# Graph layer with gathered edges: block 0's messages before the weight set-up, and b_e as the opening pass of the edge products

## The chip, the cores and the metric

One Trainium2 chip, of which the program uses one core. The metric is device time in microseconds for one execution of the whole program. Three timed runs of the kernel before are shown; a fourth execution was taken with the hardware profiler and is the one that all rows of the profile come from.

## The reference, cut to what matters

Nodes: N = 8192 rows of C = 256. Edges: E = 131072, sorted by destination, each with 64 attributes. In a few lines:

```python
ea  = edge_attr @ w_e + b_e                      # 131072 x 256
msg = relu(x[src] + ea)                          # one gathered row of x for each edge
agg = segment_sum(msg, dst, num_segments=8192)
t   = x + agg
h_local = bn(relu(t @ w1 + b1) @ w2 + b2 + x)
h_attn  = bn(attention(x in 256 groups of 32 nodes, 4 heads) @ out_w.T + out_b + x)
out = h_local + h_attn
out = bn(out + relu(out @ m_w1 + m_b1) @ m_w2 + m_b2)
result = layernorm(x + out)
```

Everything is float32.

## The kernel before, in words

**Edge blocks.** The edges are cut into NB = 128 blocks of 1024. A block passes through these steps:

- `gather(b)` (issue at L138): eight indirect DMAs from GpSimd's queue (POOL), one for each 128 edges. They write the rows `x[src]` into the tile `xs`, of which there are four buffers. The indices of blocks 0 and 1 lie in the small tile `srcd`, those of all later blocks in `srci`, which is made in the set-up (L193 to L198).
- `load_edges(b)` (L154): four loads of edge attributes into `ea` from SyncE's queue (SP), two buffers. `edge_transpose(b)` (L169, VectorE) turns them into `eaT`, two buffers.
- `edge_products(b)` (L459 and L467, TensorE): `edge_attr @ w_e`, in two halves of one `pe` tile each. A `pe` tile takes two banks of PSUM; the index `i` of the code selects both the bank and which 64 partitions of `eaT` and `w_e` the product is taken over. In the blocks below NX = 20 a second set of matmuls, L467, adds `b_e`: its stationary operand `sel` has ones in row 0 and in row 64 and zeros elsewhere, and its moving operand is `be`. From block 20 on, the gathers read `xb` instead, a copy of x to which `b_e` has been added, and L467 is left out.
- `edge_messages(b)` (L487 VectorE, L491 ScalarE): `msg = relu(pe + xs)`. When L487 has read `xs`, its buffer is free for `gather(b + 4)`.
- `edge_hot`, `edge_sums` (L496, L510), `edge_place` (L528, L538): the sum over destinations by matmuls with one-hot operands.

**Nodes.** 16 chunks of 512 nodes. `attention_front` loads `xn` (L276), transposes it (L283) and makes q and k (L294); `attention_back` and `dense` (L308 to L444) do the rest. The copy `xb` is made in blocks 0 to 14 of the loop: SyncE loads `xp`, VectorE adds `b_e` (L558), SyncE stores it (L559).

**Order.** The program text fixes the order on TensorE everywhere, and on VectorE and ScalarE in the first NV = 26 blocks. The loop over pairs of blocks takes, for the pair (b, b+1): the gathers of blocks b+2 and b+3; products and messages of b; the sums of the pair before; products and messages of b+1; then steps of the node streams, dealt out by assumed costs (`PER_X` = 4.2 and `PER` = 5.1 for each block). Before the loop stands the set-up: the loads of indices and weights, their transposes (L197 to L266), and the transposes of the first two node chunks. Matmuls of block 0 come after all of that. The last 24 blocks are ordered by a table of arrival times, `came`, which assumes 10.06 us for each block.

**Queues.** Loads of `w_e`, `b_e`, `in_w` and `out_w` are issued by ScalarE (L179 to L188), all others by SyncE. As built, the loads from SyncE and ScalarE share eight semaphores in turn, so a load is issued only when the eighth load before it has landed; the gathers have eight of their own, in the same way.

Of the kernel before, what the change touches and what calls it, by code (L numbers as in the profile page):

```python
# [9 lines left out]
FP = mybir.dt.float32  # L10
I32 = mybir.dt.int32
AF = mybir.ActivationFunctionType
ALU = mybir.AluOpType
# [40 lines left out]
def gnn_kernel(ctx: ExitStack, tc: tile.TileContext, x, src, dst, edge_attr, w, out):  # L54
# [72 lines left out]
    def bank2():  # L127
        return pps.tile([P, 2, CH], FP, name="pe", tag="pe", bufs=2)
# [31 lines left out]
    load_edges(0)  # L160
    gather(1)
    load_edges(1)
# [3 lines left out]
    def edge_transpose(b):  # L166
        ea = ea_of.pop(b)
        eaT = eaT_of[b] = epool.tile([P, NH * EQ, QR], FP, name="eaT", tag="eaT", bufs=2)
        nc.vector.transpose(eaT, ea[:, QR:].rearrange("p (g d) -> p g d", d=ED)[:, :, :QR])  # L169

    with tc.tile_pool(name="setup", bufs=1) as sp:


        srci_r = npool.tile([P, BE], I32, name="srci_r", tag="y")
        dsti_r = npool.tile([P, BE], I32, name="dsti_r", tag="h1")
        nc.sync.dma_start(srci_r, src.rearrange("(s e) -> s e", s=NB))
        nc.sync.dma_start(dsti_r, dst.rearrange("(s e) -> s e", s=NB))
        for h in range(2):
            nc.scalar.dma_start(we[h * ED : (h + 1) * ED, :], w["w_e"])  # L179
        nc.scalar.dma_start(be, w["b_e"][None, :].to_broadcast([P, C]))  # L180
        in_r = npool.tile([P, 3 * KC, C], FP, name="in_r", tag="m1")
        out_r = npool.tile([P, KC, C], FP, name="out_r", tag="vn")
        nc.scalar.dma_start(in_r, w["in_w"].rearrange("(o p) c -> p o c", p=P))
# [4 lines left out]
        nc.scalar.dma_start(out_r, w["out_w"].rearrange("(o p) c -> p o c", p=P))  # L188
        for b in range(2):
            edge_transpose(b)  # L190
            load_edges(b + 2)
        srcf = npool.tile([P, NH * TJ, EQ, QR], FP, name="srcf", tag="zT")
        nc.vector.tensor_copy(srcf, srci_r.rearrange("s (t r m) -> s t m r", r=QR, m=EQ))  # L193
        for h in range(NH):
            ps = bank()[:, : TJ * NB].rearrange("p (j s) -> p j s", j=TJ)
            for j in range(TJ):
                nc.tensor.transpose(ps[:, j, :], srcf[:, h * TJ + j].rearrange("s m r -> s (m r)"), ident)  # L197
            nc.vector.tensor_copy(srci[:, :, h * TJ : (h + 1) * TJ].rearrange("p s j -> p j s"), ps)  # L198

# [74 lines left out]
    def attention_front(n0, st, pool, bank):  # L274
        xn = st["xn"] = pool.tile([P, TN, C], FP, name="xn", tag="xn", bufs=4)
        nc.sync.dma_start(xn, x[ds(n0, CH), :].rearrange("(t p) c -> p t c", p=P))  # L276
        yield REST
# [170 lines left out]
    chunk = [{} for _ in range(NCH)]  # L448
    pe_of, msg_of, oh_of, newest = {}, {}, {}, {}

    def edge_products(b):

        eaT = eaT_of.pop(b).rearrange("p (h m) r -> p h (m r)", h=NH)
        for h in range(0, NH, 2):
            pe = bank2().rearrange("p i (u c) -> p i u c", u=2)
            for u in range(2):
                for i in range(2):
                    rows = slice(i * ED, (i + 1) * ED)
                    nc.tensor.matmul(  # L459
                        pe[:, i, u, :], eaT[rows, h + u], we[rows, :],  # L460
                        start=(b >= NX or u == 0), stop=(b >= NX), skip_group_check=True,
                    )
            if b < NX:
                for u in range(2):
                    for i in range(2):
                        rows = slice(i * ED, (i + 1) * ED)
                        nc.tensor.matmul(  # L467
                            pe[:, i, u, :], sel[rows, :], be[rows, :], start=False, stop=True, skip_group_check=True
                        )
            pe_of[b, h] = pe  # L470

    def next_edges(b):
        if b < NB:
            edge_transpose(b)
        if b + 2 < NB:
            load_edges(b + 2)

    def edge_messages(b):

        xs = xs_of.pop(b)  # L480
        msg = msg_of[b] = epool.tile([P, NH, TJ, C], FP, name="msg", tag="msg", bufs=3)
        n = 2 if b < NB - 1 else 1
        for h in range(0, NH, 2):
            pe = pe_of.pop((b, h))
            for u in range(0, 2, n):
                hs = slice(h + u, h + u + n)
                nc.vector.tensor_add(  # L487
                    msg[:, hs].rearrange("p u i c -> p i u c"), pe[:, :, u : u + n, :],
                    xs[:, hs].rearrange("p u i c -> p i u c"),
                )  # L490
                nc.scalar.activation(msg[:, hs], msg[:, hs], AF.Relu)  # L491

    def edge_hot(b):

        oh = oh_of[b] = epool.tile([P, TB, WN], FP, name="oh", tag="oh", bufs=2)
        nc.vector.tensor_tensor(  # L496
            oh,
            iota_n[:, None, :WN].to_broadcast([P, TB, WN]),
            rel[:, b, :, None].to_broadcast([P, TB, WN]),
            ALU.is_equal,  # L500
        )

    def edge_sums(blocks):

        pw = pps.tile([P, 2, C], FP, name="pw", tag="pw", bufs=1)
        for i, b in enumerate(blocks):
            msg, oh = msg_of.pop(b), oh_of.pop(b)
            for j in range(TJ):
                for h in range(NH):
                    nc.tensor.matmul(  # L510
                        pw[h * WN : (h + 1) * WN, i, :], oh[:, h * TJ + j, :], msg[:, h, j, :],
                        start=(j == 0), stop=(j == TJ - 1), skip_group_check=True,
                    )
        n = len(blocks)
        ws = epool.tile([P, 2, C], FP, name="ws", tag="ws", bufs=2)
        newest["ws"] = nc.scalar.copy(ws[:, :n], pw[:, :n]).ins  # L516
        oh2 = epool.tile([P, 2, WB], FP, name="oh2", tag="oh2")
        for i, b in enumerate(blocks):
            nc.vector.tensor_scalar(oh2[:, i, :], iota_n, wrow[:, b : b + 1], None, ALU.is_equal)
        return blocks, ws, oh2  # L520

    def edge_place(blocks, ws, oh2):

        l2 = pps.tile([P, KC, C], FP, name="l2", tag="pw", bufs=1)
        last = len(blocks) - 1
        for i in range(last + 1):
            for k in range(KC):
                nc.tensor.matmul(  # L528
                    l2[:, k, i * NPB : i * NPB + WB], ws[:, i, k * P : (k + 1) * P], oh2[:, i, :],
                    start=(i == 0 and k == 0), stop=(i == last), skip_group_check=True,  # L530
                )
        n = blocks[0] * NPB - WL
        end = n + last * NPB + WB
        for c in range(max(n, 0) // CH, (min(end, N) - 1) // CH + 1):
            assert chunk[c]["v"]
            a, z = max(n, c * CH), min(end, (c + 1) * CH)
            xT = chunk[c]["xT"][:, :, a - c * CH : z - c * CH]
            newest["xT"] = nc.vector.tensor_add(xT, l2[:, :, a - n : z - n], xT).ins  # L538

# [86 lines left out]
    with tc.manual_schedule(engines={PE}):  # L626
# [9 lines left out]
        for c in range(NCH):  # L636
            st, before, same = chunk[c], chunk[c - 1], chunk[c - 4]
            front = attention_front(c * CH, st, npool, bank)
            if c < 2:
                next(front)  # L640
                next(front)
# [23 lines left out]
        while b < TAIL:  # L665
# [10 lines left out]
            edge_products(b)  # L676
            next_edges(b + 2)
            edge_messages(b)
# [188 lines left out]
```

## Time and profile before

| | us |
|---|---|
| timed runs | 1328.47, 1331.11, 1333.70 |
| median | 1331.11 |
| the profiled execution | 1331.09 |
| its span, first to last instruction | 1329.3 |
| TensorE busy in the span | 1195.2 (90%) |
| GpSimd busy | 983.9 (74%) |
| VectorE busy | 784.9 (59%) |
| ScalarE busy | 587.7 (44%) |
| mean granted TensorE clock | 0.967 |

How to read it: all rows of the profile count time from the first instruction of the span, and the profiled execution adds 1.8 us around the span. In a row of the timeline the first number is the start, the second the time from there to the end of the row, both in us, then come the engine, the line of the kernel, the operation, output and input, shapes and count; in brackets stands the idle time of the engine just before and what ended it. "issue" means that the engine waited for nothing that the profile shows. A float32 matmul leaves two matmul records and two weight loads. The share of busy time of an engine tells little here, since the set-up, the blocks below 20, the long middle and the end have different limits.

### The profile page before, as it was taken

The numbers are of one execution on the slowest core, as the hardware profiler recorded it, in microseconds if no ns is written. First come the engines' busy times: TensorE is split into PE (matmuls) and PEld (weight loads), VectorE is DVE, ScalarE is ACT, GpSimd is POOL, SyncE is SP. The second block draws the span as 40 slices with busy tenths as digits, with TensorE's granted clock in tenths as the row PEclk, the third lists the DMA queues.
The fourth block names the chain that finished last, engine by engine and source line by source line (L and its number), as shares of the span: only waits on it lengthen the run. The fifth ranks groups of instructions, "written<-read, shape, count | busy, mean of one in ns | idle before, by whom it ended". The sixth has DMA issues, their size and how long they took to land.

```text
span 1329.3 us, 21099 instructions
## 1 busy us (share of the span) xinstructions
PE 1195.2 (90%) x7795; PEld 741.0 (56%) x7795; DVE 784.9 (59%) x1339; ACT 587.7 (44%) x840; POOL 983.9 (74%) x1032
## 2 busy tenths in 40 slices
PE   2898989999998989899898988989898999999987
PEld 1566656556555556555555555545555555545655
DVE  4377555765756565755647465465646557575654
ACT  1343433454536454443435444354454444443433
POOL 6677777777777777777777777777777777777771
PEclk9899999999999989999999999989899999999998
DMA  7999966676667666666756666566566466656741
GB/s 204 320 267 299 260 199 169 169 199 167 181 160 196 157 181 167 171 177 165 190 150 185 160 176 171 157 181 167 170 169 199 138 169 186 166 163 159 192 129 47
DMA packets 148904, 240.34 MB, mean 181 GB/s; under 512 B 27934, under 2 KB 112188, under 8 KB 148028
## 3 DMA queue, kind: packets, MB, share of 16 engines
q0 software_dynamic: 49152, 134.28, 37.6%
q1 hardware_dynamic: 97196, 103.34, 28.9%
q10 hardware_dynamic: 2448, 1.32, 0.4%
q8 instruction: 63, 1.03, 0.3%
q14 instruction: 45, 0.37, 0.1%
HBM read 222.06 MB, written 16.78 MB: 180 GB/s over the span
## 4 chain that ended last, share of the span: by engine, by line
PE 38%; POOL 28%; issue 14%; DVE 9%; DMA 8%; ACT 2%; DVEq 0%; ACTq 0%; SPq 0%; POOLq 0%
POOL xs L138 28%; PE at L391 11%; PE pe L459 8%; DMA xs<-xb,srci 5%; PE at L294 5%; PE pw L510 4%; DVE msg L487 3%; PE l L528 3%; PE at L372 2%; PE pe L467 2%; PE at L308 1%; DMA xp<-in_x_dram 1%; PE at L360 1%; PE pe L325 1%; DMA in_r<-in_L_gnn_in_w_dram 1%
## 5 line engine op out<-in xcount | busy, mean ns | idle before, releaser
L138 POOL DMA_INDIRECT xs<-xb,srci x864 | 823.7, 953 | 263.2 <-issue 250.1
L491 ACT ACTIVATE msg<-msg 128x1024 f32<-128x1024 f32 (+1 forms) x258 | 270.0, 1049 | 435.5 <-DVE msg L487 432.6
L487 DVE TENSOR_TENSOR msg<-pe,xs 128x1024 f32<-128x1024 f32 (+1 forms) x258 | 305.7, 1199 | 155.4 <-DMA xs<-xb,srci 88.6
L459 PE MATMUL pe<-we,eaT 64*128 64x256 f32 x2048 | 271.0, 398 | 29.8 <-DVE msg L487 26.4
L459 PEld LDWEIGHTS pe<-we,eaT 64*128 64x128 f32 x2048 | 192.1, 191 | 118.5 <-issue 74.6
L138 POOL DMA_INDIRECT xs<-in_x_dram,srci x144 | 143.0, 993 | 48.8 <-issue 39.6
L169 DVE STREAM_TRANSPOSE eaT<-ea 128x512 f32<-128x512 f32 x128 | 90.1, 704 | 99.6 <-PE pe L459 70.9
L510 PE MATMUL pw<-msg,oh 128*32 128x256 f32 x2048 | 130.4, 389 | 6.6 <-DVE oh L496 5.0
L391 PE MATMUL at<-hA,mw 128*128 128x512 f32 (+2 forms) x304 | 123.9, 538 | 2.9 <-DVE hA L401 2.2
L294 PE MATMUL at<-xT,inT 128*128 128x512 f32 x256 | 120.9, 598 | 0.4 <-ACT xT L284 0.4
L391 PE MATMUL at<-m,mw 128*128 128x512 f32 (+2 forms) x304 | 117.5, 529 | 2.5 <-ACT qk L297 2.2
L510 PEld LDWEIGHTS pw<-msg,oh 128*32 128x32 f32 x2048 | 60.4, 111 | 69.1 <-issue 30.7
L528 PEld LDWEIGHTS l<-oh,ws 128*128 128x128 f32 x512 | 78.0, 196 | 28.4 <-issue 21.9
L528 PE MATMUL l<-oh,ws 128*128 128x160 f32 x512 | 87.9, 312 | 2.0 <-ACT ws L516 2.0
L391 PEld LDWEIGHTS at<-hA,mw 128*128 128x128 f32 x304 | 54.7, 196 | 50.5 <-issue 42.6
L391 PEld LDWEIGHTS at<-m,mw 128*128 128x128 f32 x304 | 54.2, 190 | 49.9 <-issue 44.5
L538 DVE TENSOR_TENSOR xT<-l,xT 128x96 f32<-128x96 f32 (+4 forms) x107 | 46.1, 452 | 54.2 <-PE l L528 53.9
L294 PEld LDWEIGHTS at<-xT,inT 128*128 128x128 f32 x256 | 47.0, 190 | 55.3 <-issue 51.0
L391 PE MATMUL at<-xT,w 128*128 128x512 f32 (+2 forms) x152 | 70.9, 606 | 6.9 <-DVE xT L538 6.9
L407 ACT ACTIVATE m<-at,vec 128x512 f32<-128x512 f32 (+2 forms) x76 | 46.8, 616 | 57.2 <-PE at L391 56.7
L297 ACT ACTIVATE qk<-at,vec 128x512 f32<-128x512 f32 x64 | 43.6, 684 | 62.6 <-PE at L294 62.4
L391 PE MATMUL at<-h,w 128*128 128x512 f32 (+2 forms) x152 | 64.2, 544 | 6.1 <-ACT h L398 6.1
(107 smaller groups left out, 1199.9 us busy)
## 6 DMA issues: line engine op xcount, KB each, us to landing
ea<-in_edge_attr_dram SPq DMA_DIRECT2D x512, 128.0 KB
xs<-xb,srci POOLq DMA_INDIRECT x864
xn<-in_x_dram SPq DMA_DIRECT2D x16, 512.0 KB
out_dram<-y SPq DMA_DIRECT2D x14, 512.0 KB
xp<-in_x_dram SPq DMA_DIRECT2D x10, 512.0 KB
xb<-xp SPq DMA_DIRECT2D x10, 512.0 KB
xp<-in_x_dram SPq DMA_DIRECT2D x3, 1024.0 KB
xb<-xp SPq DMA_DIRECT2D x3, 1024.0 KB
```

Source lines behind the costliest of these rows:

```text
L138: nc.gpsimd.indirect_dma_start(out=xs[:, h, j, :], out_offset=None, in_=x if b < NX else xb[:, :], in_offset=bass.IndirectOffsetOnAxis(ap= ...
L169: nc.vector.transpose(eaT, ea[:, QR:].rearrange("p (g d) -> p g d", d=ED)[:, :, :QR])
L294: nc.tensor.matmul(ps, inT[:, k, o * P : (o + 1) * P], xT[:, k, :], start=(k == 0), stop=(k == KC - 1))
L297: nc.scalar.activation(qk[:, o, :], ps, AF.Identity, bias=v_("in_b", o))
L391: nc.tensor.matmul(ps, wt[:, k, o * P : (o + 1) * P], act[:, k, :], start=(k == 0), stop=(k == nk - 1))
L407: nc.scalar.activation(m1[:, o, :], layer(mw1, KC, o, hA), AF.Relu, bias=v_("m_b1", o))
L459: nc.tensor.matmul(pe[:, i, u, :], eaT[rows, h + u], we[rows, :], start=(b >= NX or u == 0), stop=(b >= NX), skip_group_check=True,)
L487: nc.vector.tensor_add(msg[:, hs].rearrange("p u i c -> p i u c"), pe[:, :, u : u + n, :], xs[:, hs].rearrange("p u i c -> p i u c"),)
L491: nc.scalar.activation(msg[:, hs], msg[:, hs], AF.Relu)
L510: nc.tensor.matmul(pw[h * WN : (h + 1) * WN, i, :], oh[:, h * TJ + j, :], msg[:, h, j, :], start=(j == 0), stop=(j == TJ - 1), skip_group_ ...
L528: nc.tensor.matmul(l2[:, k, i * NPB : i * NPB + WB], ws[:, i, k * P : (k + 1) * P], oh2[:, i, :], start=(i == 0 and k == 0), stop=(i == la ...
L538: newest["xT"] = nc.vector.tensor_add(xT, l2[:, :, a - n : z - n], xT).ins
```

## The change

Five things change; the work computed is the same.

1. **Block 0 ahead of the weights.** `edge_products(0)`, `next_edges(2)` and `edge_messages(0)` are taken out of the loop and put into the set-up, after `srci` is made and before the transposes of `in_w`. For this the functions on edges are moved up in the file, unchanged but for `edge_products`.
2. **Order of loads.** All set-up loads are now issued by SyncE, in this order: `src`, the edges of block 0, `w_e`, the edges of block 1, `b_e`, `dst`, twelve small vectors, `in_w`, chunk 0 of x, `out_w`, chunk 1 of x, edges of blocks 2 and 3.
3. **Set-up on VectorE.** The index conversion (`srcf`, four copies to `srci`) now stands ahead of `edge_transpose(0)` and `(1)`. VectorE's two adds of block 0's messages stand between the steps that prepare `dst`.
4. **Chunks 0 and 1 of x** are loaded by a new function `load_nodes`, ahead of their transposes.
5. **b_e first, in passes of 512 columns.** In a half of a block below 20, `b_e` opens the sum with one matmul of 512 columns for each 64 partitions (`be` repeated twice by a step of zero), and the four products of 256 columns are added to it. Before, four products of 256 columns opened it, and four `b_e` matmuls of 256 columns closed it.

```diff
     gather(0)
-    load_edges(0)
     gather(1)
-    load_edges(1)
...
+    def edge_products(b):
+        eaT = eaT_of.pop(b).rearrange("p (h m) r -> p h (m r)", h=NH)
+        for h in range(0, NH, 2):
+            pe = bank2().rearrange("p i (u c) -> p i u c", u=2)
+            half = [slice(i * ED, (i + 1) * ED) for i in range(2)]
+            if b < NX:
+                for i, rows in enumerate(half):
+                    nc.tensor.matmul(
+                        pe[:, i], sel[rows, :], be[rows, None, :].to_broadcast([ED, 2, C]), start=True, stop=False, skip_group_check=True
+                    )
+            for u in range(2):
+                for i, rows in enumerate(half):
+                    nc.tensor.matmul(
+                        pe[:, i, u, :], eaT[rows, h + u], we[rows, :], start=(b >= NX), stop=True, skip_group_check=True
+                    )
+            pe_of[b, h] = pe
...
         srci_r = npool.tile([P, BE], I32, name="srci_r", tag="y")
+        nc.sync.dma_start(srci_r, src.rearrange("(s e) -> s e", s=NB))
+        load_edges(0)
         dsti_r = npool.tile([P, BE], I32, name="dsti_r", tag="h1")
-        nc.sync.dma_start(srci_r, src.rearrange("(s e) -> s e", s=NB))
+
+        for h in range(2):
+            nc.sync.dma_start(we[h * ED : (h + 1) * ED, :], w["w_e"])
+        load_edges(1)
+        nc.sync.dma_start(be, w["b_e"][None, :].to_broadcast([P, C]))
         nc.sync.dma_start(dsti_r, dst.rearrange("(s e) -> s e", s=NB))
-        for h in range(2):
-            nc.scalar.dma_start(we[h * ED : (h + 1) * ED, :], w["w_e"])
-        nc.scalar.dma_start(be, w["b_e"][None, :].to_broadcast([P, C]))
...
-        nc.scalar.dma_start(in_r, w["in_w"].rearrange("(o p) c -> p o c", p=P))
...
-        nc.scalar.dma_start(out_r, w["out_w"].rearrange("(o p) c -> p o c", p=P))
-        for b in range(2):
-            edge_transpose(b)
-            load_edges(b + 2)
+        nc.sync.dma_start(in_r, w["in_w"].rearrange("(o p) c -> p o c", p=P))
+        load_nodes(0, chunk[0], npool)
+        nc.sync.dma_start(out_r, w["out_w"].rearrange("(o p) c -> p o c", p=P))
+        load_nodes(CH, chunk[1], npool)
         srcf = npool.tile([P, NH * TJ, EQ, QR], FP, name="srcf", tag="zT")
...
+        for b in range(2):
+            edge_transpose(b)
+            load_edges(b + 2)
+        edge_products(0)
+        next_edges(2)
+        edge_messages(0)
...
-            edge_products(b)
-            next_edges(b + 2)
-            edge_messages(b)
+            if b:
+                edge_products(b)
+                next_edges(b + 2)
+                edge_messages(b)
             if waiting:
                 sums = edge_sums(waiting)
```

GpSimd's order is the same in both programs, and from block 1's messages on, VectorE's and ScalarE's are too. TensorE's differs in the place of block 0's products and in the shape and place of the `b_e` matmuls.

## The prediction

> **What bounds the kernel now.** The page's costliest groups come first, since the share of busy time misleads: TensorE has 90%, but is it the one that everything waits for?
>
> ```profile
> L138 POOL DMA_INDIRECT xs<-xb,srci x864 | 823.7, 953 | 263.2 <-issue 250.1
> ...
> L138 POOL DMA_INDIRECT xs<-in_x_dram,srci x144 | 143.0, 993 | 48.8 <-issue 39.6
> ```
>
> A gather keeps GpSimd 0.95 us and the next follows 0.30 us later, with nothing waited for ("issue"). So gathers come every 1.25 us, and 1024 of them from 4.25 us (the first start in the timeline) would start the last at 1283.0 undisturbed. In the timeline it starts at 1302.79, so 19.8 us went to disturbances on GpSimd; the last gather's landing (1306.5), the last block and the tail bring the span to 1329.3. The list of who waited for whom, for GpSimd, divides them:
>
> ```profile
> POOL xs L138 <- issue: 297.0, 967, 2.6
> POOL xs L138 <- DVE msg L487: 6.9, 13, 3.2
> POOL xs L138 <- DMA xs<-xb,srci: 3.3, 11, 0.3
> POOL xs L138 <- DVE oh L519: 2.6, 4, 1.7
> ...
> POOL xs L138 <- DVE srci L198: 0.9, 1, 0.9
> ```
>
> Only three waits are longer than the usual 0.30: 3.2, 1.7 and 0.9 us. The timeline shows where (three places, in order of time):
>
> ```profile
> 23.06 1.07 DVE L193 CAST srcf<-srci_r 128x1024 f32<-128x1024 int32 x1 [1.24 <-DMA srci_r<-in_src_dram]
> 23.16 1.80 POOL L138 DMA_INDIRECT xs<-in_x_dram,srcd  x1 [0.30 <-issue]
> ...
> 25.87 1.47 POOL L138 DMA_INDIRECT xs<-in_x_dram,srci  x1 [0.92 <-DVE srci L198]
> ...
> 49.30 0.94 POOL L138 DMA_INDIRECT xs<-in_x_dram,srci  x1 [3.22 <-DVE msg L487]
> ...
> 197.06 0.96 POOL L138 DMA_INDIRECT xs<-in_x_dram,srci  x1 [1.68 <-DVE oh L519]
> ```
>
> The first is the index of block 2; the second is gather(4), which needs the buffer that block 0's messages free; the third is gather(18), freed by block 14's messages (they end at 196.8). After 197 nothing holds the gathers but small stretchings. From there on time saved on GpSimd moves the end one for one: the chain has waits for gathers at 1169.9, 1272.5 and 1302.8, so TensorE is tied to arrivals in the tail too.
>
> Between 48 and 330 us, though, TensorE works nearly without a gap, behind the gathers. Its timeline in this stretch, for a block with b_e and one without:
>
> ```profile
> 60.49 1.13 PE L459 MATMUL pe<-we,eaT 64*128 64x256 f32 x8
> 61.46 1.03 PE L467 MATMUL pe<-be,sel 64*128 64x256 f32 x8
> 62.32 1.03 PE L459 MATMUL pe<-we,eaT 64*128 64x256 f32 x8
> 63.19 1.03 PE L467 MATMUL pe<-be,sel 64*128 64x256 f32 x8
> 64.15 1.93 PE L510 MATMUL pw<-msg,oh 128*32 128x256 f32 x32
> ...
> 249.09 2.00 PE L459 MATMUL pe<-we,eaT 64*128 64x256 f32 x16
> 251.02 1.93 PE L510 MATMUL pw<-msg,oh 128*32 128x256 f32 x32
> ```
>
> From start to start: 3.66 us with b_e (16 matmuls), 1.93 without (8).
>
> **The change, part by part.**
>
> *Index load first.* `src` was issued at 15.26 and landed at 23.04. Now it is SyncE's first large load, at about 2.7; 512 KB at the 200 to 270 GB/s of the first 15 us take about 2.5 us, so it lands near 7 and the indices are ready near 11 (conversion 1.1, transposes 2.1, copies), 13 us before gather 16 at 24.3. The wait beyond the usual 0.30 goes: -0.62 us. The stretching does not go by itself: 1.80 and 1.47 instead of 0.95, so 1.37 us, beside the two conversions of 1.07 us on VectorE. The Trainium skill ("SBUF — State Buffer", "SBUF: two separate sides") says that GpSimd cannot write descriptors while VectorE holds their shared port, and so the operation delays the gather by what is left of it. By the row a conversion cost 0.85 and 0.52, by the rule up to 1.07; both conversions remain, now beside gathers that wait for nothing else. So I count 0 for them; ends -1.4 (both fall into pauses) and +0.8.
>
> *Block 0 early.* Its products need `b_e` (the twelfth load: 1.8 MB lie ahead of or in it, some 10 us at the measured rate beside gathers, near 13) and the transposed edges (near 12). Four us of matmuls, 8 at half clock, then VectorE's adds, placed after the four 1.2 us steps on `dst`: done by 24 to 30. gather(4) can start at 44.3 plus stretching. The wait goes with 14 us to spare: -2.92. The next two blocks are no new wait if TensorE is half a us earlier than before: block 1's messages ended at 53.9 and gather(5) will want them at about 55.9; block 2's ended at 66.4 and gather(6) will want them at 65.9.
>
> *TensorE's start.* The transposes of x waited for their load (2.75 and 0.65 us) and ran from 37.8 to 42.3; then came 5.8 us of block 0's products and a wait, up to 48.0. The 5.8 us go out of the loop. The x loads now stand ahead of the edges of blocks 2 and 3, but behind 3.0 MB of set-up loads from one queue, eight in flight; at some 165 GB/s (270 less the gathers' 105, 128 KB each 1.25 us), the second chunk lands near 31. What comes before on TensorE (`in_w`, near 24, then 27 transposes, and VectorE's chain behind block 0's adds) lasts till 32 to 36. I take 34: 3.8 us earlier. Together TensorE is 9.6 us earlier at block 1 (ends 5.8 and 11.6). Moving four loads from ScalarE's to SyncE's queue costs issue time only (0.43 to 0.6 us each), inside these figures.
>
> *b_e in passes of 512.* The columns streamed are the same, half as many weight loads. The Trainium skill ("TensorE: Matmul & The Clock Gate", "Part 3: Packing small matmuls") says that tiles on different rows run side by side, a group taking one matmul's time plus about 4 ns per tile: then the change costs 0 (and the loss of weight loads gives 0, as they are hidden). The row says a little else: 8 matmuls take 1.93 and 16 take 3.66, which is 9 and 17 steps of 0.215. So a matmul is two passes, one after the other on its own rows, and only the second pass lies beside the next matmul's first. Put into the new order: b_e passes of 0.43 end at 0.86 (rows 0 to 63) and 1.28 (rows 64 to 127); the first product fits beside the last b_e pass, but the second starts at 1.28, and the half ends at 1.92 instead of 1.73. That is +0.19 a half, +0.39 a block. I take the row. Between blocks 1 and 14 the products of 8 and 12 lie beside VectorE's longer chains (TensorE idles 5.0 and 4.65 us there), so 12 blocks count: +4.6 us at block 14.
>
> *Block 14.* gather(18) was ready 1.38 us before its buffer. GpSimd now comes 3.54 us earlier, so block 14's messages must be 4.92 earlier for a full gain. They are 9.6 - 4.6 = 5.0 earlier: just enough, and -1.38 more. Block 12 had 0.2 us to spare and needs 3.3; it has 5.8. If the start of TensorE is the late end, they are 1.2 earlier, and all gain but 1.2 is lost there.
>
> *xb.* Its last store was issued at 203.5, and gather(20), the first to read it, started at 217.1; both move earlier by about 5.
>
> *Sum.* -0.62 - 2.92 - 1.38 = -4.92, against the profiled 1331.09: 1326.2. The median of the runs, 1331.11, is the same within 0.02.
>
> **The rivals.**
>
> A, as summed: 1326.2, and 1324 to 1328 with the ends of the conversions and a us of noise. For it: three named waits, each with its cause moved. Chance 0.58.
>
> B, the buffer wait moves to block 12 or 14: TensorE starts only 6 to 8 us earlier, the 4.6 us of staggered passes eat it, and gather(18) gains 1.2 to 3. Then 1328 to 1330; I say 1329. For it: the margin of 0.1 us. Chance 0.2.
>
> C, slower: passes of 512 columns do not lie beside each other at all. Then b_e takes four passes of 0.43 in a half, 1.71 instead of 0.86: +1.7 a block, 20 us over 12 blocks, less 9.6: gather(18) is held 10 us longer than before, 1341. It turns from gain to loss at 9.6 / 12 = 0.8 us a block. Against it: the 256-column rows do overlap. Chance 0.1 (1334 to 1346).
>
> D, more than I count: both conversions fall into pauses, and the `xp` adds of blocks 2 to 14, beside which gathers take up to 2.29 us, hit fewer of them: 1323. Chance 0.12.
>
> That the change doesn't do what it says is ruled out by the order of instructions, which shows block 0's matmuls ahead of the `in_w` transposes.
>
> **How the numbers follow.** Predicted 1326.2. For 8 in 10 the range takes A and B and most of D, and leaves out C and the far ends: 1322.5 to 1331.5. Half a per cent is 6.7 us, about what a measurement of this kernel tells from no change, so faster means below 1324.4 and slower above 1337.8. A gives faster 0.14 of its 0.58, D all 0.12: 0.26. C gives slower 0.1. The rest, 0.64, lies within.
>
> **What would show it.** The wait of 3.22 us at gather(4) and the 0.92 at block 2's index are gone, and gather(4) starts at 45 to 46. The two conversions still stretch a gather each. A block with b_e takes 4.0 to 4.1 us from its first matmul to the sums, not 3.66; if 3.5 to 3.7, the stagger is wrong. The transposes of x start at 32 to 36. gather(18) has a wait of no more than 0.3 (A) or one of 1 to 4 us (B). The last gather starts near 1298, and the tail behind it is still 26.5 us. A new wait of GpSimd for its own earlier gathers, with loads crowding the first 40 us, would make me wrong in a way that I have not priced.

## The result, and the profile after

| | before | after |
|---|---|---|
| median of the timed runs, us | 1330.47 (14 runs) | 1326.82 (14 runs) |
| lowest and highest | 1328.34 to 1333.70 | 1320.81 to 1329.44 |
| ratio after / before, 95% | | 0.9969 (0.9958 to 0.9980) |
| the profiled execution | 1331.09 | 1320.81 |
| its span | 1329.3 | 1319.0 |

The median fell by 3.65 us, where 4.92 was predicted. The profiled execution of after is the lowest of its 14; the spans of the other 13 are 1324.3 to 1327.7. So its trace may hold a gain of the change, and a gain that only this execution had.

The list of costliest groups of after has the same two groups of gathers, with a mean of 951 and 988 ns (before 953 and 993):

```profile
L138 POOL DMA_INDIRECT xs<-xb,srci x864 | 821.5, 951 | 263.2 <-issue 244.4
...
L138 POOL DMA_INDIRECT xs<-in_x_dram,srci x144 | 142.3, 988 | 43.9 <-issue 38.7
```

The list of GpSimd's waits in after (total, number, longest) is where the change shows. The waits of 3.2, 1.7 and 0.9 us have left it; beside the time before the very first gather (2.6) no wait is longer than the usual 0.3. Its first rows:

```profile
POOL xs L138 <- issue: 290.2, 945, 2.6
POOL xs L138 <- DMA xs<-xb,srci: 7.0, 23, 0.3
POOL xs L138 <- DVE msg L205: 2.7, 9, 0.3
```

The timeline of after, in order of time: the two conversions (VectorE), each with the gather beside it; a third stretched gather, beside the subtraction on `dst` that follows; the second half of block 0's messages; the transposes of x; gather(4); block 14's messages; and gather(18):

```profile
6.86 1.55 POOL L138 DMA_INDIRECT xs<-in_x_dram,srcd  x1 [0.30 <-issue]
7.22 1.07 DVE L288 CAST srcf<-srci_r 128x1024 f32<-128x1024 int32 x1 [3.68 <-DMA srci_r<-in_src_dram]
...
16.22 1.41 POOL L138 DMA_INDIRECT xs<-in_x_dram,srcd  x1 [0.30 <-issue]
...
16.41 1.09 DVE L335 CAST dstf<-dsti_r 128x1024 f32<-128x1024 int32 x1 [1.30 <-DMA dsti_r<-in_dst_dram]
...
20.44 1.52 POOL L138 DMA_INDIRECT xs<-in_x_dram,srcd  x1 [0.30 <-issue]
...
23.00 1.23 DVE L205 TENSOR_TENSOR msg<-pe,xs 128x1024 f32<-128x1024 f32 x1
...
29.70 2.91 PE L387 MATMUL at<-ident,xn 128*128 128x128 f32 x16
...
46.03 0.95 POOL L138 DMA_INDIRECT xs<-in_x_dram,srci  x1 [0.30 <-DVE vn L419]
...
184.32 2.31 DVE L205 TENSOR_TENSOR msg<-pe,xs 128x1024 f32<-128x1024 f32 x2
...
192.18 0.95 POOL L138 DMA_INDIRECT xs<-in_x_dram,srci  x1 [0.30 <-issue]
```

Block 14's messages in before:

```profile
194.47 2.32 DVE L487 TENSOR_TENSOR msg<-pe,xs 128x1024 f32<-128x1024 f32 x2
```

Set beside the rows of before, gather(2) does not start earlier at all (26.01, before 25.87), though its wait is gone: three stretches of 0.60, 0.46 and 0.57 us stand ahead of it. gather(4) starts 3.27 us earlier (49.30 before) and gather(18) 4.88 earlier (197.06 before). gather(20) starts at 212.19, where it started at 217.06. The two traces can be read as a ledger:

| part of the span | after minus before, us |
|---|---|
| up to gather(20): waits gone, -4.92; stretched gathers, about 0 | -4.87 |
| gather(20) to the last gather (1295.72, before 1302.79): fewer stretched gathers | -2.20 |
| last gather to the end of the span: 23.3 instead of 26.5 | -3.2 |
| sum | -10.3 |

Stretched means what gathers took over 0.95 us, added up: after block 20 it was 6.7 us before and 4.5 after. The third row has a cause of its own. Each trace is cut here 0.7 to 0.8 us ahead of the start of its last gather; after the two times, the columns are the length, TensorE's busy time and matmul records, its granted clock, the DMA share and GB/s. Below are the message add that waits for the last gather (VectorE), and the last block's sums (TensorE). First before:

```profile
1302.00:1329.30 27.30, 17.75 (x124) 0.84 0.11 35
...
1306.62 0.69 DVE L487 TENSOR_TENSOR msg<-pe,xs 128x512 f32<-128x512 f32 x1 [1.17 <-DMA xs<-xb,srci]
...
1308.84 1.94 PE L510 MATMUL pw<-msg,oh 128*32 128x256 f32 x16
```

and after:

```profile
1295.00:1319.00 24.00, 15.23 (x126) 0.92 0.13 40
...
1298.98 0.66 DVE L205 TENSOR_TENSOR msg<-pe,xs 128x512 f32<-128x512 f32 x1
...
1300.69 1.07 PE L228 MATMUL pw<-msg,oh 128*32 128x256 f32 x16
```

In before the rows of the last gather were waited for: the add that reads them began 3.83 us after the gather's start, in after 3.26 us after it and without a wait. TensorE stood still for 2.06 us meanwhile, and then ran at a granted clock of 0.50: the 16 matmul records of the last block's sums took 1.94 us, where after has 1.07. So the sums began 6.05 us after the last gather's start instead of 4.97, and from there the next steps, up to the dense matmuls at 1314.34 and 1303.88, took 5.5 us instead of 3.2. No edit of the change stands in this part of the program. Rows two and three, 5.4 us, are of the size by which the profiled execution lies below its own median (6.0), so I put them down to the two executions, and only the first row, 4.87, to the three waits. That fits the measured ratio (2.7 to 5.6 us less), but the first experiment shows that it is not the only reading.

### The profile page after: what moved, and what is told of

It is laid out like the page before. It is cut to its first block, busy times and chain, and to the rows that moved or that the text cites. A ratio compares the mean times of both kernels' runs of the same rounds, so it can differ in the third digit from the quotient of the medians.

```text
span 1319.0 us, 20794 instructions
## 1 busy us (share of the span) xinstructions
PE 1192.2 (90%) x7635; PEld 725.2 (55%) x7635; DVE 786.4 (60%) x1339; ACT 586.8 (44%) x840; POOL 981.8 (74%) x1032
## 4 chain that ended last, share of the span: by engine, by line
PE 42%; POOL 26%; issue 13%; DMA 9%; DVE 8%; ACT 2%; DVEq 0%; SPq 0%; POOLq 0%; ACTq 0%
POOL xs L138 26%; PE at L495 13%; PE pe L185 8%; DMA xs<-xb,srci 6%; PE at L398 5%; PE pw L228 4%; PE l L246 3%; DVE msg L205 3%; PE at L476 3%; PE at L412 2%; PE pe L180 2%; DMA xs<-in_x_dram,srci 1%; PE at L464 1%; DVE bd L456 1%; PE pe L429 1%
## 5 line engine op out<-in xcount | busy, mean ns | idle before, releaser
L185 PEld LDWEIGHTS pe<-we,eaT 64*128 64x128 f32 x2048 | 195.5, 191 | 118.6 <-issue 79.1
L495 PE MATMUL at<-xT,w 128*128 128x512 f32 (+2 forms) x152 | 66.6, 575 | 6.9 <-DVE xT L256 6.9
```

What stands on the lines that cost most here:

```text
L185: nc.tensor.matmul(pe[:, i, u, :], eaT[rows, h + u], we[rows, :], start=(b >= NX), stop=True, skip_group_check=True)
L495: nc.tensor.matmul(ps, wt[:, k, o * P : (o + 1) * P], act[:, k, :], start=(k == 0), stop=(k == nk - 1))
```

## The experiments

In the first eleven runs the kernel before took about 2000 to 2036 us beside them, because operations began some us after what they needed was done; these times say nothing of a kernel at 1330 us, so of these runs only stretches ahead of the disturbance, and stretches inside one engine's unbroken work, are used. What the disturbance looks like comes last in this part. The twelfth run was taken with before at 1327.89.

### Block 0 back in the loop (undisturbed)

```diff
         for b in range(2):
             edge_transpose(b)
             load_edges(b + 2)
-        edge_products(0)
-        next_edges(2)
-        edge_messages(0)
...
-            if b:
-                edge_products(b)
-                next_edges(b + 2)
-                edge_messages(b)
+            edge_products(b)
+            next_edges(b + 2)
+            edge_messages(b)
```

> Again the changed kernel with block 0's products and messages back in the loop. If operations hand over as in the first two profiles (kernel before near 1330): theory 1 (a buffer that is free before its gather costs nothing) says no index wait, x transposes near 30, block 0's messages at 37 to 40 and no wait over 0.3 at gather(4) near 46; block 14's messages 5.8 us later than in the changed kernel, so gather(18) waits 0.2 to 0.5 and the ratio is 0.997. Theory 2 (the early messages of block 0 were needed) says a wait of 2 us or more at gather(4) or gather(18) and 0.999. If the kernel before is near 2000 again, every gather(4) waits over 5 us as in the other such runs and neither is decided.

Median 1325.50 (10 runs) against 1327.89 (13 runs): ratio 0.9982 (0.9968 to 0.9996). Its timeline: the transposes of x, block 0's products and messages, block 1's products, the projections of chunk 0, then gather(4), block 14's messages and gather(18):

```profile
30.61 2.00 PE L384 MATMUL at<-ident,xn 128*128 128x128 f32 x16
...
32.54 1.13 PE L180 MATMUL pe<-be,sel 64*128 64x512 f32 x4
...
36.94 2.32 DVE L205 TENSOR_TENSOR msg<-pe,xs 128x1024 f32<-128x1024 f32 x2
...
38.27 1.82 PE L180 MATMUL pe<-be,sel 64*128 64x512 f32 x4 [2.02 <-DVE msg L205]
...
43.60 7.13 PE L395 MATMUL at<-xT,inT 128*128 128x512 f32 x16
...
45.65 0.94 POOL L138 DMA_INDIRECT xs<-in_x_dram,srci  x1 [0.30 <-DVE msg L205]
...
193.92 2.31 DVE L205 TENSOR_TENSOR msg<-pe,xs 128x1024 f32<-128x1024 f32 x2
...
196.50 0.97 POOL L138 DMA_INDIRECT xs<-in_x_dram,srci  x1 [3.89 <-DVE oh L237]
```

Both theories are half right. gather(4) starts at 45.65 without a wait, although block 0's messages stand in the loop: the other edits (the order of the loads and of the index set-up) bring the x transposes to 30.6 and the end of these messages to 39.3, 6 us ahead of gather(4). So the wait of 2.92 us did not need the move of block 0. The kernel with that move alone (below) has no wait at gather(4) either; each of the two would have been enough. But gather(18) now waits 3.89 us, since block 14's messages end at 196.2 instead of 186.6: block 0's matmuls cost the loop 7.4 us at its start (the q and k projections of chunk 0 begin at 43.60; in the changed kernel at 36.18; 3.6 are block 0's matmuls, 2.0 a wait of block 1's products for the message adds, and 1.7 by which block 1's products are slower, 5.3 instead of 3.6) and 9.6 at block 14, where I expected 5.8. What GpSimd had gained, it gives back there: gather(20) starts at 216.71, 0.35 earlier than before. In these traces the move of block 0 pays for gather(18); for gather(4) it is one of two edits that would have done.

One thing stays open here, and it bears on the whole account. By its gathers up to gather(20) this kernel should be 0.4 us faster than before (0.7 at the last gather), and it measured 2.4 faster (0.5 to 4.2); the intervals of this ratio and of the changed kernel's overlap. So the times do not show that the move of block 0 pays, and the first row of the ledger alone does not give this kernel's gain. Its tail is 22.8 us, like that of after. Either the 26.5 us of before's profile were usual for before, and part of the gain lies in the tail, or they were not, and the gain of this kernel has a source that its trace doesn't show. One trace of each kernel can't decide it. Nor can both rows of the changed kernel's ledger hold in full for its medians: the first and the third together are 8.1 us, above its interval.

### b_e passes of 512: alone, and issued twice

The first kernel is before with only the new `edge_products`, run twice:

> One part of the change alone: b_e opens the sums in passes of 512 columns; all else as in the kernel before. The changed kernel's trace shows 3.64 us for a block with b_e (3.66 before). Theory 1: 0.02 us a block, 0.3 us at block 14, so the wait of gather(18) shrinks from 1.7 to some 1.4, that of gather(4) stays at 3.2: no difference in time within 0.5 us. The prediction's staggered passes: +0.39 a block, the wait of gather(18) grows to 6 us, +4 to +5 us. Rival (half the weight loads make TensorE faster): gather(18) no longer waits, -1.4 us.

> The kernel before with only the new b_e passes. Theory 1: the two row halves run side by side in passes of 512 too, a block takes 3.64 us from its first matmul to the sums as before, gather(18) waits 1.7 as before and gather(20) starts at 217: ratio 1.000. Rival (staggered passes, as in the prediction): 4.05 us a block, gather(18) waits 5 to 6 us, ratio 1.0035. Second rival (half as many weight loads let TensorE gain): gather(18) waits under 0.5 and the ratio is 0.999.

The second is the changed kernel with this edit:

```diff
             if b < NX:
-                for i, rows in enumerate(half):
-                    nc.tensor.matmul(
...
+                for again in range(2):
+                    for i, rows in enumerate(half):
+                        nc.tensor.matmul(
```

> The changed kernel with the b_e matmuls of 512 columns issued twice in each half of a block below 20 (the second opens the sum anew and overwrites the first). If passes of 512 on two times 64 rows run side by side, each block takes 2 times 0.86 more: 5.36 us instead of 3.64. Theory 1: block 14's messages had 5.5 us to spare; 12 to 13 blocks between 1 and 14 bring 20.6 to 22 us, so gather(18) comes 15 to 17 us later, the time is about 1342 (ratio 1.009), and GpSimd's wait list shows it as waits for buffers. Rival: TensorE has much more slack there, since VectorE sets the pace of the blocks below 20; then 1327 to 1332.

The times (1992.13 and 2029.49, ratios 0.9939 and 0.9995; 2057.23, ratio 1.013) are disturbed. But a block's matmuls follow each other on one engine, and where no event broke in, their pitch can be read. A block below 20 in the second run of the b_e kernel, from its first matmul to the sums (L507):

```profile
145.99 1.13 PE L459 MATMUL pe<-be,sel 64*128 64x512 f32 x4
146.96 1.03 PE L464 MATMUL pe<-we,eaT 64*128 64x256 f32 x8
147.82 1.02 PE L459 MATMUL pe<-be,sel 64*128 64x512 f32 x4
148.68 1.03 PE L464 MATMUL pe<-we,eaT 64*128 64x256 f32 x8
149.64 0.64 PE L507 MATMUL pw<-msg,oh 128*32 128x256 f32 x8
```

That is 3.65 us. The undisturbed trace of after has 3.64 for block 1 (32.54 to 36.18):

```profile
32.54 1.13 PE L180 MATMUL pe<-be,sel 64*128 64x512 f32 x4
...
35.22 1.03 PE L185 MATMUL pe<-we,eaT 64*128 64x256 f32 x8
36.18 1.12 PE L398 MATMUL at<-xT,inT 128*128 128x512 f32 x2
```

With b_e issued twice it is 5.36:

```profile
145.00 1.99 PE L181 MATMUL pe<-be,sel 64*128 64x512 f32 x8
146.82 1.03 PE L186 MATMUL pe<-we,eaT 64*128 64x256 f32 x8
147.68 1.88 PE L181 MATMUL pe<-be,sel 64*128 64x512 f32 x8
149.40 1.03 PE L186 MATMUL pe<-we,eaT 64*128 64x256 f32 x8
150.36 1.93 PE L229 MATMUL pw<-msg,oh 128*32 128x256 f32 x32
```

So a pair of b_e matmuls on two times 64 rows costs 0.86 us (1.72 more for two pairs). A single matmul of 512 columns over all 128 rows takes 0.87 in the same trace of after (eight of them, the projections of chunk 0, from 36.18 to 43.15), so the two row groups run side by side in passes of 512 columns, as they do in passes of 256. Staggered passes (4.05 a block) and passes one after the other (5.4) are both refuted, and half as many weight loads gain nothing (3.64 and 3.65 us a block against 3.66). How much spare time TensorE has at block 14 was not measured by this, since its time is disturbed.

### The conversions, and what else holds up GpSimd

The changed kernel with `nc.scalar.copy` in place of `nc.vector.tensor_copy` for `srcf` and `dstf`:

> The changed kernel with the two conversions of index arrays from integer to float (srcf and dstf) on ScalarE instead of VectorE. Theory 1 (a conversion on VectorE holds up GpSimd, as the two stretched gathers of 1.55 and 1.41 us at 6.9 and 16.2 suggest): both gathers take 0.95 instead, so gathers from 17 us on start 1.0 to 1.1 us earlier; the time falls by that at most where GpSimd sets the end. Rival (the stretches come from the loads that run at the same time): they stay, and nothing moves. The subtraction of lo from dstf at 19.9 stays on VectorE, and beside it the gather of 1.52 stays.

Its first 21 us are ahead of the disturbance. The conversions start at 6.95 and 16.23 on ScalarE; the gathers beside them, and the gather at the subtraction:

```profile
6.98 0.95 POOL L138 DMA_INDIRECT xs<-in_x_dram,srcd  x1 [0.30 <-issue]
...
17.01 0.95 POOL L138 DMA_INDIRECT xs<-in_x_dram,srcd  x1 [0.30 <-issue]
...
20.77 1.94 POOL L138 DMA_INDIRECT xs<-in_x_dram,srcd  x1 [0.30 <-issue]
```

Both stretches are gone (6.86 and 16.22 in after), and the eleventh gather comes 12.68 us after the first instead of 13.72: 1.04 earlier. The conversion itself takes 1.99 us on ScalarE instead of 1.07. The gather at 20.77 lies beside the subtraction of `lo` (both inputs in SBUF), which stayed on VectorE, and took 1.94, where after has 1.52. By block 2 the gain, counted from the first gather, is 0.6 us. The time (2012.80, ratio 0.9887) is disturbed; whether this version beats the changed kernel at 1327 us was not measured.

Then the gathers alone, beside strings of equal operations:

> Only the 1024 gathers (all from x), with the indices made as in the changed kernel; messages, sums, node work and the copy of x are left out. Beside the gathers run strings of 90 equal operations, one string after the other and waited for by nobody: ScalarE's conversion, then on VectorE the conversion, the reduction (lo), the xp add (both inputs in SBUF), the message add (one input in PSUM), the edge transpose, a copy out of PSUM. Theory 1 (GpSimd's own pace sets the gathers, and certain VectorE operations hold it up): 1.25 us for each gather where nothing runs or ScalarE runs; beside conversions and xp adds 1.7 to 2.5; beside message adds, reductions, transposes and copies out of PSUM 1.25 to 1.35. In all about 1283 to 1400 us. Rival (stretches come from the loads beside): 1.25 everywhere, and the last gather starts at 1283 to 1286.

One execution took 1453.58 us. From about 490 us on, VectorE's operations fall into a pitch of 1.40 us (below); the gathers have it too from 494 to 517, beside the last xp adds, and from 553 on. So the strings before 490 are read, and of the message adds only the gathers between 520 and 540. The timeline at the start of the conversions (188.40), and at the start of the xp adds (400.70):

```profile
187.80 0.95 POOL L85 DMA_INDIRECT xs<-in_x_dram,srci  x1 [0.30 <-issue]
189.05 1.68 POOL L85 DMA_INDIRECT xs<-in_x_dram,srci  x1 [0.30 <-issue]
191.04 1.91 POOL L85 DMA_INDIRECT xs<-in_x_dram,srci  x1 [0.31 <-issue]
...
401.09 1.65 POOL L85 DMA_INDIRECT xs<-in_x_dram,srci  x1 [0.30 <-issue]
403.04 0.95 POOL L85 DMA_INDIRECT xs<-in_x_dram,srci  x1 [0.31 <-issue]
404.30 0.95 POOL L85 DMA_INDIRECT xs<-in_x_dram,srci  x1 [0.30 <-issue]
```

| beside the gathers | a gather every, us | a gather takes, us |
|---|---|---|
| ScalarE's conversions (20 to 180 us) | 1.253 | 0.95 |
| VectorE's conversions (200 to 280) | 2.211 | 1.91 |
| VectorE's reductions (300 to 400) | 1.253 | 0.95 |
| VectorE's xp adds (420 to 480) | 1.260 | 0.96 |
| VectorE's message adds, one each 1.40 us (520 to 540) | 1.253 | 0.95 |

The rival, stretches from the loads, is refuted for conversions: there were hardly any loads here (105 GB/s beside ScalarE's string, nearly all of it the gathers'). Beside the string of conversions a gather comes with every second conversion (2 times 1.106 us), and takes 0.96 us longer. An xp add stretched its first gather by 0.70 too, but then add and gather fell into step, with both at a pitch of 1.26 us, and cost nothing. My 1.7 to 2.5 for xp adds was wrong for a string; in the kernel the adds come singly, so each can hold one gather up (after has 2.52 at 58.5, beside an xp add of 128x2048). Transposes and copies out of PSUM came too late to be read. 1024 gathers at 1.253 us are 1283 us: with 4.2 ahead of them and a tail of 23, GpSimd's own pace would give 1310 (an estimate from these rows and the tail of after).

### Eight more gathers

```diff
     gather(0)
+    gather(0)
     gather(1)
```

> The changed kernel with the gathers of block 0 issued twice: eight more indirect DMAs, at the front of GpSimd's queue. Theory 1 (GpSimd's gathers set the end): each costs 1.25 us to the end, 10.0 us in all, so 1336.8, ratio to the kernel before 1.0045. The later blocks' gathers have no wait over 0.3. Theory 2 (TensorE sets the end, and the gathers have slack): no more than 2 us.

> Again the changed kernel with the gathers of block 0 issued twice, eight more at the front of GpSimd's queue, now for its trace. Theory 1 (GpSimd's gathers set the end): every later gather starts 10.0 us later than in the changed kernel (8 times 1.25), the last at about 1306, no wait over 0.3 at blocks 2, 4 and 18, and one execution takes 1331 to 1337. Theory 2 (TensorE sets the end and the gathers have slack): the last gather's start moves by less than 3 us. If handing over between engines takes several us, as in the runs near 2000 us, the trace decides nothing of this.

2034.82 (ratio 1.002), and 2004.60 in a single execution (before 2003.41): disturbed. In the first run 48 gathers go out at 1.25 us up to 63.99, so gather(5) could have started at 65.2, where after has 56.01: 9.2 us later, that is 10.0 less some stretches. In the second the last of the 48 starts at 65.22, which makes 10.5. Then gather(5) waits 20.4 and 16.3 us for messages that the disturbance delays. That a gather at the front of the queue costs 1.25 us there is seen; that it costs so much at the end of the kernel isn't.

### The parts alone, disturbed

Three edits: the changed kernel with block 0 back in the loop (the diff above; twice), the kernel before with only block 0's functions moved ahead of the weights, and before with only the load of `src` and its conversion first.

> Undoes one part of the change: block 0's products and messages go back into the loop, the new order of loads and the new b_e passes stay. Theory 1 (the chain of gathers on GpSimd sets the end; TensorE only has to free the buffers in time): x is loaded early now, so its transposes still start near 29, block 0's messages end near 37, and gather(4), due at 46, does not wait. Block 14's messages come some 5 us later than in the changed kernel (186.6 there), near 191.5, just before gather(18) wants its buffer at 192.2. So gather(20) starts at 212 to 213 and the time is that of the changed kernel: 1326 to 1328. Theory 2 (what counts is how early and how briefly TensorE does its work in the blocks below 20): 4 to 5 us are given back, 1331.

> The changed kernel with block 0's products and messages put back into the loop; the loads, the earlier indices and the new b_e passes stay. Theory 1 (the chain of gathers sets the end, and any buffer that comes free before its gather costs nothing): no index wait at block 2; the x transposes start near 30, so block 0's products start near 33 and its messages end near 41, ahead of gather(4) at 46, so no wait over 0.3 there either; block 14's messages come 5.8 us later than in the changed kernel, at about 192.4, so gather(18) waits 0.2 to 0.5. Time 4 us below the kernel before: ratio 0.997. Theory 2 (block 0's early messages were needed for the gather(4) gain): gather(4) waits 2 us or more and the ratio is 0.999.

> One part of the change alone: block 0's products and messages move into the set-up behind the index transposes; loads and b_e passes are those of the kernel before. Theory 1: the wait for the index stays (0.9 us), gather(4) does not wait (-2.9), block 14 is some 5 us earlier so that gather(18) doesn't wait either (-1.4): gather(20) starts near 212.8, and the time is 4.3 us below the kernel before, 1326. Rival: without the early loads block 0's messages are late themselves (the index step on VectorE ends at 28) and TensorE's set-up is pushed back, so block 14 waits as before: -2.9 at most, 1327.5 to 1330.

> One part of the change alone: the index list is loaded first and converted ahead of the edge transposes; the rest as in the kernel before. Theory 1 (a wait on one chain is given back at the next that is still there): the wait of 0.9 us for the index goes, but gather(4) still needs block 0's messages, which end near 49; its wait grows from 3.2 to about 3.8 and nothing is gained: gather(20) at 216.5 to 217.5, time as before. Rival (waits add up): -0.6 us, which shows in gather(20)'s start, 216.4, more than in the time.

Times and ratios: 1998.03 (0.9995) and 2028.36 (0.9983); 1993.49 (0.9963); 2000.10 (0.9997). With block 0 in the loop, gather(4) waits 14.4, 15.1 and 13.7 us for messages that the disturbance delays, so nothing on gather(4) and gather(18) follows; for the first kernel the undisturbed run above stands in. What lies ahead of the disturbance: with `src` loaded first, the conversion starts at 6.73 and block 2's gathers wait for nothing, so the index wait goes by that edit alone. With only block 0 moved, its messages end at 33.2, and gather(4) does not wait for them, in spite of the disturbance:

```profile
49.10 0.95 POOL L138 DMA_INDIRECT xs<-in_x_dram,srci  x1 [0.30 <-issue]
```

(gather(5) is the first to wait, 6.5 us.) But the conversion of `srcf` stood behind block 0's first message add (24.86) on VectorE, started at 26.00 instead of 23.06, and block 2's index was waited for by 4.58 us, partly by the disturbance. So, without the earlier load of `src`, block 0 gets in the way of the index.

A fifth buffer for `xs`, another way to attack the waits for buffers, was not tried.

### What the disturbance looks like

In the run with more gathers, ScalarE copies one tile of `in_r` after another, each time after two transposes on TensorE (0.7 us):

```profile
55.33 0.37 ACT L312 COPY inT<-at 128x256 f32<-128x256 f32 x1 [27.22 <-remote]
60.93 0.37 ACT L312 COPY inT<-at 128x256 f32<-128x256 f32 x1 [5.23 <-remote]
...
66.53 0.37 ACT L312 COPY inT<-at 128x256 f32<-128x256 f32 x1 [4.27 <-remote]
```

These three come 5.60 us apart (the next follows after 4.90); in after two of these copies took 0.63 us together, with nothing between. The transposes that the second one needs had ended at 56.45, 4.5 us before it began. "remote" marks an operation whose releaser is not found in the trace. It is weak evidence here, since these traces hold fewer records of semaphore events: 9,100 to 9,400 in the ten full kernels, where the undisturbed ones hold 28,700 to 28,800. In the run of gathers alone, VectorE's transposes wait for nobody, and still:

```profile
673.43 0.71 DVE L131 STREAM_TRANSPOSE eaT<-ea 128x512 f32<-128x512 f32 x1 [0.69 <-DVE eaT L131]
674.83 0.71 DVE L131 STREAM_TRANSPOSE eaT<-ea 128x512 f32<-128x512 f32 x1 [0.69 <-DVE eaT L131]
```

A pitch of 1.400 us, a quarter of 5.60; the gathers beside them have the same pitch, and keep it after VectorE has finished. In the full kernels the gathers still go out every 1.25 us where their buffers are free. I know of nothing in the programs with this period and take it that the pace came from outside them; what set it is not shown.

## Why the prediction was right, and where its steps were not

**The bound.** Right as far as the traces show. In after no gather but the very first waits more than the usual 0.3 us, and gathers without any other work keep the same 1.253 us. That a us saved on GpSimd is a us at the end is not shown: the runs with more gathers are disturbed, and with block 0 in the loop the time gained more than the gathers did.

**Index load first, -0.62.** Right for the wait, in cause and size: `src` landed at 7.2 (7 predicted), the copies to `srci` ended at 11.2 (11), and the wait is gone.

**The conversions, counted at 0.** Right: 0.60 and 0.46 us of stretching instead of 0.85 and 0.52. The mechanism held as well: moved to ScalarE, the conversions stretch nothing. Not foreseen was the third stretch, 0.57 us beside the subtraction on `dst`: in before the same operation (at 30.16) stretched none. With it the gathers ahead of block 2 gained nothing; up to gather(20) all stretches together are the same in both traces, within 0.1 us. The rule of the Trainium skill that I used ("SBUF — State Buffer", "SBUF: two separate sides") gives up to the length of the operation, and the strings show 0.96 of 1.07 us in the steady case. The section says it of the modes in which VectorE takes both ports; which mode a conversion ran in, no run shows.

**Block 0 early, -2.92 at gather(4).** The size was right (gather(4) at 46.03, block 0's messages done at 24.2), but the cause named is only one of two. "The wait goes with 14 us to spare" is true (it came out at 22), and the move alone removes the wait; but with block 0 in the loop the wait also goes, with 6 to spare. I priced it against the one edit that moves block 0, and not against the other edits that bring TensorE's set-up forward, the loads of x among them, which I had put into another paragraph.

**TensorE's start.** Mis-sized. The transposes of x started at 29.70, not 34 and outside 32 to 36; TensorE began the projections of chunk 0 15.5 us earlier than before (51.70 to 36.18), outside my 5.8 to 11.6. Of these 15.5, block 0's products and wait are 5.8, as predicted. The transposes started 8.1 earlier instead of 3.8, and took 2.8 us instead of 4.5 (1.6): there was no wait between the chunks (0.65), and the granted clock, 0.50 throughout before, was 0.50 for the first half and 1.00 for the rest. `in_w` was there at 23.2, as said (24); the term at fault is what "lasts till 32 to 36" behind it: 8 to 12 us in my sum, 6.5 in the trace. And the second chunk of x was not late at 31: all 16 transposes ran on from 29.70 without a wait.

**b_e in passes of 512, +4.6 us at block 14.** Wrong, 0 instead: 3.64 us a block, as in before (3.66). I read 1.93 and 3.66 as 9 and 17 half steps, and took the odd step for a stagger that comes again at each change of shape. It comes once in a stretch of 64-row matmuls, however long: 4 pairs of 0.43 are 1.72 and 8 are 3.44, each with 0.2 on top, and the doubled b_e passes (12 times 0.43, 5.16) took 5.36. By the rows about half of it lies at the first group of a stretch and half at the last (0.96 or 0.97 us from start to start, the groups between 0.86). Two durations could not tell the two readings apart, and the side-by-side rule of the Trainium skill that I set aside ("TensorE: Matmul & The Clock Gate", "Part 3: Packing small matmuls") gave the right value. The row itself was fine; my model of it was not the only one that fits it.

**Block 14, "just enough".** The gain of 1.38 came, but not by a margin of 0.1; here the sum was right by luck. Block 14's messages are 10.15 us earlier (184.32; 194.47 before) and end 5.5 us ahead of gather(18). The two errors above have the same sign here; together they would have made it 15.5, and 5.3 of that was lost on the way to block 14 (the lead of the messages is 14.7 at block 1, 13.0 at block 8, 11.7 at block 12). About 3.5 us of the loss are longer waits of TensorE (its list of waits adds up to 13.1 us from there to block 14 in before, and to 16.6 in after); why they grew, no experiment shows. Block 12 had hardly any room, not the 0.2 us of my reading: its messages ended at 174.38, gather(16) started at 174.68, and gather(4) and gather(18) started 0.26 us after the messages that they waited for. It changes nothing, since block 12's messages are 11.7 us earlier. Rival B was near, though: without the move of block 0 gather(18) waits 3.89 us, as in the first experiment.

**The tail, unchanged.** The predicted 26.5 us came out as 23.3 in the one trace, by the later rows of the last gather and the half clock in before's. Whether tails of 26.5 us are usual for before is open. Rival D, 1323, looks right if only the profiled execution is read; the median says A, 1326.82, and D's reasons did not happen: both conversions stretched a gather, and between gather(4) and gather(18) the stretches are 6.1 us, before 6.3.

**The sum.** -4.92 predicted, -4.87 in the trace at gather(20), -3.65 in the medians; the interval of the ratio, 2.7 to 5.6 us, holds both and decides no closer. So the three waits are gone in the trace by causes that the parts bear out. That they, and not the tail or the later gathers, are what the median gained is argued and not shown.

## What to carry to other kernels

When several edits stand ahead of the same wait, ask for each one alone whether the wait would already be gone; here the early block, and the other edits without it, would each have emptied the wait at gather(4), and what the early block added was the slack for a later one. Where one engine issues at a fixed pace, its own list of waits, cut at the last long one, is the budget of any change to the order of work: three waits worth 4.92 us were what such a change could win up to block 20. And compare a ledger of a profiled execution with the medians before believing its last rows: here 10.3 us in the traces stand against 3.65 in the medians, so most of the last 5.4 can't belong to the kernels.

## What the runs showed of the hardware

- A conversion from int32 to float32 on VectorE (1.07 us for 128x1024) holds up a gather of GpSimd: in after the two gathers beside conversions ended 0.12 and 0.13 us after them, and in a string a gather came every 2.211 us instead of 1.253. Adds with both inputs in SBUF hold up the first gather (1.65 us), then run in step with the gathers at 1.26 us. Reductions, the same conversion on ScalarE (1.99 us), and adds with one input in PSUM (one each 1.40 us) held up none: 1.253 us.
- Two matmuls of 512 float32 columns on two times 64 rows take 0.86 us together, a single one over 128 rows 0.87; a stretch of 64-row matmuls costs 0.2 us more, whether it has 1.72, 3.44 or 5.16 us of them.
- A pause of TensorE of 2.06 us in the tail of before was followed by a granted clock of 0.50 (16 matmul records in 1.94 us instead of 1.07); pauses of 0.77 and 1.08 us at the same place, in after and in the first experiment, were not.
- In eleven runs operations began some us after what they needed was done: from about 24 us on in the full kernels (copies 5.60 us apart), and as a pitch of 1.400 us from about 490 us on in the kernel of gathers alone. The cause is open.
